# Cross-attention softmax of a decoder layer: a maximum that runs from group to group, one chunk in four subtracted by TensorE, scores in pairs of row strips

## The chip, the cores and the metric

The kernel runs on one NeuronCore of one Trainium2 chip, in one launch. The core has five engines that run side by side, each taking its own instructions in order: TensorE (PE, matrix products; its weight loads show as PEld), VectorE (DVE), ScalarE (ACT), GpSimd (POOL) and SyncE (SP, which issues the DMAs). PE writes its results to PSUM, a memory of eight banks of 128 x 512 floats; the other tiles lie in SBUF. Instructions on different engines wait for each other through semaphores.

The metric is device microseconds of one execution. Three executions of the kernel before took 688.26, 689.32 and 690.29 us, median 689.32.

## The reference

One decoder layer on 8 sequences of 128 tokens, width 512, all float32. Three residual blocks, each followed by a layer norm: self-attention with quantised weights, cross attention, and a gated mixture with low-rank experts. The change lies in the cross attention, whose softmax runs over an unusual axis:

```python
def proj(x, W, bias):                       # 16 heads of 32
    y = x @ W.T + bias
    return y.reshape(b, s, head_num, hd).transpose(0, 2, 1, 3).reshape(b * head_num, s, hd)
Q, K, V = proj(q, Wq, bq), proj(k, Wk, bk), proj(v, Wv, bv)
scores = jnp.einsum('bqd,bkd->bqk', Q, K) / sqrt(hd)
attn = jax.nn.softmax(scores, axis=0)       # over the 8*16 (sequence, head) pairs
res = jnp.einsum('bqk,bkd->bqd', attn, V)
```

So for each of the 128 x 128 (query, key) places, the maximum and the sum run over 128 score matrices: eight sequences times sixteen heads. Nothing can be weighed with its final factor before the last score matrix is there.

## The kernel before

The self-attention fills the first 510 us and isn't touched. After it come, in order, four stretches; the order of instructions on PE, DVE, ACT and POOL is the order in which the program emits them (it is written by hand; only SP's is left to a scheduler).

**Turning x.** `acc` holds the normalised residual, 8 tiles of 128 x 512. Loop `for t in range(B)` (L882) transposes each tile on PE (four 128 x 128 transposes into one PSUM bank, L878), ACT casts it to a high part `x1h` (L181) and DVE subtracts to get a low part `x1l` (L182): products run as three fast passes, high by high, high by low, low by high. Between the transposes stand units of the value projection (`vals`, L648; a unit is three products of 128 x 512 for one slice of 128 rows, four units and one bias product make one sequence). `VALUES_FIRST = 12` of the 32 units are placed here. The weights of the query projection arrive by DMA and are split on ACT and POOL in the same loop (`load_wq`, L863).

**Scores.** The 128 score matrices are dealt out in 32 chunks of four sequences by one head, and eight groups of four chunks. A chunk fills one PSUM bank: key position on the partitions, 4 x 128 (sequence, query position) along it. `cross_products` (L965) makes the four chunks of a group in one burst: a head has only 32 dimensions, so a product uses 32 of the array's 128 rows, and the inner loop walks over four heads in four different strips of 32 rows (L974). `cross_scores` (L982) takes the maximum of the four chunks: ACT copies the first to `top` (L991), DVE takes the maximum with the other three (L993). Then `close_group`: DVE reduces `top` over the four sequences to the group's maximum (L1080), subtracts that from each of the four chunks on the way from PSUM to SBUF (L1004), and ACT exponentiates in place (L1007). DVE also carries a running total maximum `mx` (L1085, L1087). The sums of the exponentials of the first six groups are made on POOL (L1013, L1019, L1020), those of group 6 by PE (products with the identity, L951), those of group 7 on DVE (L1013) and then PE.

The loop at L1093 interleaves this, chunk by chunk, with the units of the query projection of the next group (L693, four units a group) and with `VALUES_AT = (3, 3, 3, 3, 3, 3, 2)` units of the values. `SCORE_BANKS` names six banks, of which two are shared with those projections. A group's exponentials are relative to its own maximum; at the end factors exp(group maximum - total maximum) put them on one footing (L1038 to L1056).

**Factors and weighing.** PE adds up the sums (`lsum`, L951); DVE multiplies by the factors, reduces, takes the reciprocal (L1169 to L1171), forms one factor per group (L1174, L1319) and weighs the exponentials of sequences 0 and 1 (`weigh`, L1184), half of them on DVE, half on POOL (`WEIGH0_ON`, `WEIGH1_ON`, `WEIGH_ON = 'vvgg'`).

**Values and gate.** `for i in range(B)` with `AV_SEQ` (L1397): products of the exponentials with the values (`cross_values`, L1331), ACT copy, transpose (L1345), residual sum on DVE (L1347), layer norm (L222 to L230), transpose (L878), main product of the next block (L1208) and its gate (L1195), while sequence i + 2 is weighed. The rest is the mixture's end, not touched.

Of the kernel before, what the change touches and what calls it, by code (L numbers as in the profile page):

```python
# [49 lines left out]
VALUES_FIRST = 12  # L50
VALUES_AT = (3, 3, 3, 3, 3, 3, 2)
SCORE_BANKS = ('sc', 'tr', 'av', 'po', 'proj', 'proj')
EARLY_AT = 8
POPS = 2
LATE_GROUPS = (4, 4)
SUM_ORDER = (0, 1, 2)
DIRECT = (6,)
FACTORS_AT = (1, 2)
WEIGH0_ON = 'vvgg'
WEIGH1_ON = 'vvgg'  # L60
LADD_AT = 4
GSUM_ON = 'g'
# [14 lines left out]
WEIGH_ON = 'vvgg'  # L77
FIRST_WEIGHED = (2, 0, 3, 1)
# [52 lines left out]
BANKS = {"proj": 4, "sc": 1, "tr": 1, "av": 1, "po": 1}  # L131
# [7 lines left out]
def decoder_kernel(ctx: ExitStack, tc: tile.TileContext, a: dict, out: bass.AP):  # L139
# [5 lines left out]
    psum = {"n": BANKS_FIRST, "cm": tc.tile_pool(name="banks", bufs=1, space=PSUM)}  # L145
    psum["pool"] = psum["cm"].__enter__()

    def bank(tag, name, shape=(P, 512)):
        tag = tag if tag in psum["n"] else "turn"
        return psum["pool"].tile(list(shape), F32, tag=tag, name=name, bufs=psum["n"][tag])  # L150
# [449 lines left out]
    def open_cross():  # L600
# [47 lines left out]
        def vals(t):  # L648
# [4 lines left out]
            def part(kt):  # L653
                if kt == 0:
                    bk.append(bank("proj", f"pxv{t}"))
# [17 lines left out]
        for t in range(B):  # L673
            values_late.extend(vals(t))
# [10 lines left out]
    def x_projection(dst, m, w, x, hf, o):  # L685
        bk = []

        def part(kt):
            if kt == 0:
                bk.append(bank("proj", f"px{m}{hf}_{o}"))  # L690
# [177 lines left out]
    turn_n = [0]  # L868

    def other_bank(name, shape=(P, 512)):  # L870

        turn_n[0] += 1
        return bank(("sc", "tr", "av", "po")[turn_n[0] % 4], name, shape)
# [7 lines left out]
    wq_loads = []  # L881
    for t in range(B):  # L882
        n = VALUES_FIRST * (t + 1) // B - VALUES_FIRST * t // B
        for u in values_late[:n]:
            u()
        values_late = values_late[n:]
        if wq_loads:
            wq_loads.pop(0)()
        if t < KT:
            wq_loads.append(load_wq(t))  # L890
        tr = transposed(other_bank(f"tr_x1{t}", (P, KT, S)), t)
        hf, c = t // HALF, ts(t % HALF, S)
        split(x1[hf]["h"][:, :, c], x1[hf]["l"][:, :, c], tr[:])
    close(xr_cm)
# [4 lines left out]
    e_cm, ep = pool("e", "right")  # L899
    quads = {}  # L900

    def chunk(hf, m, rg):
        return (hf * KT + m) * 4 + rg

    def scores_of(c):

        k = c // 4
        if k not in quads:
            memory = {4: (e2, "x1h"), 5: (e2, "x1l"), 6: (xk["work"], "cl0"), 7: (xk["work"], "cl1")}
            if k in memory:  # L910
                pl, tag = memory[k]
                quads[k] = pl.tile([P, 4, HALF, S], F32, tag=tag, name=f"E{k}")
            else:
                quads[k] = ep.tile([P, 4, HALF, S], F32, tag=f"E{k}", name=f"E{k}")
        return quads[k][:, c % 4]

    xscale = 1.0 / math.sqrt(XD)  # L920
    LATE = len(LATE_GROUPS)
    EARLY = (2 * XH - sum(LATE_GROUPS)) // 4
    GROUPS = EARLY + LATE
    SIZES = (4,) * EARLY + LATE_GROUPS
    FIRST = [sum(SIZES[:i]) for i in range(GROUPS + 1)]
    gmax = ep.tile([P, EARLY, S], F32, name="gmax")
    gsum = ep.tile([P, EARLY, S], F32, name="gsum")
    lmax = ep.tile([P, 1 + LATE, S], F32, name="lmax")
    mx = ep.tile([P, S], F32, name="xmx")
    tops, lsum, sums, added, order, at_end = {}, [], {}, {}, list(SUM_ORDER), []  # L930

    def group_of(c):
        return next(i for i in range(GROUPS) if c < FIRST[i + 1])

    def max_of(gi):
        return gmax[:, gi, :] if gi < EARLY else lmax[:, gi - EARLY + 1, :]

    def late_sum(k, terms, n):

        sums.setdefault(k, (n, []))[1].extend(terms)  # L940

    def add_up():

        while order and order[0] in sums:
            k = order[0]
            n, terms = sums[k]
            if not lsum:
                lsum.append(bank("proj", "lsum", (P, 1 + LATE, S)))
            for x in terms:
                i = added[k] = added.get(k, -1) + 1  # L950
                nc.tensor.matmul(lsum[0][:, k, :], ident[:], x, start=(i == 0), stop=(i == n - 1))  # L951
            terms.clear()
            if added.get(k) != n - 1:
                return
            order.pop(0)
# [7 lines left out]
    burst = {}  # L963

    def cross_products(hf, m):  # L965


        for rg in range(4):
            c = chunk(hf, m, rg)
            burst[c] = bank(SCORE_BANKS[c % len(SCORE_BANKS)], f"xsc{c}", (P, HALF, S))  # L970
        for j in range(HALF):
            b = ts(hf * HALF + j, S)
            for rg in range(4):
                nc.tensor.matmul(  # L974
                    burst[chunk(hf, m, rg)][:, j, :],
                    xk["kT"][hf][ts(rg, XD), m, ts(j, S)],
                    qT[ts(rg, XD), m, b],
                    start=True,
                    stop=True,
                )  # L980

    def cross_scores(hf, m, rg):  # L982

        c = chunk(hf, m, rg)
        gi = group_of(c)
        i = c - FIRST[gi]
        if rg == 0:
            cross_products(hf, m)
        if i == 0:
            tops[gi] = xq.tile([P, HALF, S], F32, tag="top", name=f"top{gi}", bufs=1)  # L990
            nc.scalar.copy(tops[gi][:], burst[c][:])  # L991
        else:
            nc.vector.tensor_tensor(tops[gi][:], tops[gi][:], burst[c][:], ALU.max)  # L993

    def close_group(gi):

        c0, n = FIRST[gi], SIZES[gi]
        early, last = gi < EARLY, gi == GROUPS - 1
        direct = gi in DIRECT
        part = None if direct else ep.tile([P, HALF, S], F32, tag="part", name=f"part{gi}", bufs=1)  # L1000
        e = [scores_of(c0 + i) for i in range(n)]

        def minus(i):
            nc.vector.tensor_tensor(e[i], burst.pop(c0 + i)[:], across(max_of(gi)), ALU.subtract)  # L1004

        def exponential(i):
            nc.scalar.activation(e[i], e[i], AF.Exp, scale=xscale)  # L1007

        def add(i):
            if direct:  # L1010
                late_sum(gi - EARLY + 1, [e[i][:, j, :] for j in range(HALF)], n * HALF)
            elif i:
                (nc.gpsimd if early else nc.vector).tensor_tensor(  # L1013
                    part[:], e[0] if i == 1 else part[:], e[i], ALU.add
                )

        def total():
            if early:
                nc.gpsimd.tensor_tensor(part[:, :2, :], part[:, :2, :], part[:, 2:, :], ALU.add)  # L1019
                nc.gpsimd.tensor_tensor(gsum[:, gi, :], part[:, 0, :], part[:, 1, :], ALU.add)  # L1020
            else:
                late_sum(gi - EARLY + 1, [part[:, j, :] for j in range(HALF)], HALF)

        for i in range(n):
            minus(i)
        for i in range(2):
            exponential(i)

        at = max(soft[1], soft[2])
# [34 lines left out]
    def soon(n, f):  # L1064
        soft[0].setdefault(n, []).append(f)
# [579 lines left out]
```

## Time and profile before

The profiled execution took 690.76 us, 1.44 us above the median of the three; its span, from the first to the last instruction, is 688.9 us, so 1.9 us lie around it. The mean granted clock of TensorE in it is 0.977 of full speed.

| stretch | from | to | PE busy | DVE busy | ACT busy | POOL busy | clock |
|---|---|---|---|---|---|---|---|
| turning x | 514.5 | 532.5 | 17.96 of 18.0 | 9.92 | 8.82 | 7.34 | 1.00 |
| scores, groups 0 and 1 | 532.5 | 553.0 | 18.57 of 20.5 | 16.82 | 9.21 | 9.74 | 1.00 |
| scores, groups 2 to 4 | 553.0 | 575.0 | 19.90 of 22.0 | 19.65 | 11.67 | 14.55 | 1.00 |
| scores, groups 5 to 7 | 575.0 | 590.0 | 12.63 of 15.0 | 14.48 | 7.88 | 10.79 | 0.83 |
| sums, factors, weighing | 590.0 | 606.0 | 8.33 of 16.0 | 15.48 | 3.54 | 6.54 | 0.71 |
| values and gate, first five | 606.0 | 640.0 | 30.86 of 34.0 | 19.20 | 13.06 | 21.09 | 0.86 |

Times are us from the start of the span. How to read it: an engine that is busy for nearly the whole of a stretch may set its length, but a matmul's record reaches on into the next one's start (records of 0.39 us begin 0.23 us apart), so a busy PE is less full than it looks. The clock column is the share of full speed that the hardware granted to the array; 0.71 is a mean of pieces at 1.00 and pieces at 0.50. What ends a stretch is read from the chain of waits, in which each piece of work is followed back to what released it.

### The profile page before, as it was taken

The numbers are of one execution on the slowest core, as the hardware profiler recorded it, in microseconds if no ns is written. First come the engines' busy times: TensorE is split into PE (matmuls) and PEld (weight loads), VectorE is DVE, ScalarE is ACT, GpSimd is POOL, SyncE is SP. The second block draws the span as 40 slices with busy tenths as digits, with TensorE's granted clock in tenths as the row PEclk, the third lists the DMA queues.
The fourth block names the chain that finished last, engine by engine and source line by source line (L and its number), as shares of the span: only waits on it lengthen the run. The fifth ranks groups of instructions, "written<-read, shape, count | busy, mean of one in ns | idle before, by whom it ended". The sixth has DMA issues, their size and how long they took to land.

```text
span 688.9 us, 11383 instructions
## 1 busy us (share of the span) xinstructions
PE 647.6 (94%) x3476; PEld 489.1 (71%) x3476; DVE 518.4 (75%) x1319; ACT 465.5 (68%) x1181; POOL 466.2 (68%) x452
## 2 busy tenths in 40 slices
PE   6899899999999999999999999989999988579996
PEld 3787677778787777777777877757767665556652
DVE  4978676778777878788787877876894899965465
ACT  3478889987898888897888878867114455223433
POOL 4655977978879788797797887976033477366514
PEclk9999999999999999999999999989999999669999
DMA  8664432433433334343332431443001001100003
GB/s 286 182 180 116 113 84 70 108 95 89 108 92 93 85 102 93 79 111 100 78 84 47 139 77 47 114 186 115 1 0 31 1 1 62 35 2 1 1 0 123
DMA packets 31775, 57.36 MB, mean 83 GB/s; under 512 B 4831, under 2 KB 7135, under 8 KB 31714
## 3 DMA queue, kind: packets, MB, share of 16 engines
q1 hardware_dynamic: 31714, 56.64, 29.7%
q8 instruction: 27, 0.44, 0.3%
q14 instruction: 34, 0.28, 0.1%
HBM read 33.55 MB, written 2.10 MB: 52 GB/s over the span
## 4 chain that ended last, share of the span: by engine, by line
PE 73%; DVE 11%; POOL 7%; ACT 4%; issue 3%; DMA 1%; SPq 0%; POOLq 0%; DVEq 0%; ACTq 0%
PE ps L316 20%; PE po L452 15%; PE sc L383 7%; PE av L422 7%; PE ps L302 4%; PE tr L414 3%; PE pf L1208 3%; PE pxk L693 3%; PE pxv L657 2%; POOL q L351 2%; DVE top L993 2%; PE pxq L693 2%; POOL sw L350 1%; DVE E L1004 1%; PE tr_x L878 1%
## 5 line engine op out<-in xcount | busy, mean ns | idle before, releaser
L316 PE MATMUL ps<-xh,w 128*128 128x512 f32 x336 | 157.0, 467 | 0.0
L326 DVE SCALAR_TENSOR_TENSOR part<-ps,scales,part 128x512 f32<-128x512 f32 x168 | 125.7, 748 | 28.9 <-ACT part L322 19.1
L316 PE MATMUL ps<-xl,w 128*128 128x512 f32 x336 | 132.4, 394 | 0.0
L461 ACT ACTIVATE po<-po,ratios 128x512 f32<-128x512 f32 x162 | 105.0, 660 | 39.1 <-PE po L452 38.1
L349 POOL TENSOR_TENSOR t<-x,tables 128x512 f32<-128x512 f32 x70 | 90.2, 1289 | 40.6 <-DVE x L326 36.2
L452 PE MATMUL po<-ch,wo 128*128 128x512 f32 x256 | 113.7, 444 | 1.8 <-ACT accT L463 1.4
L350 POOL TENSOR_TENSOR sw<-sw,tables 128x512 f32<-128x512 f32 x71 | 92.1, 1297 | 20.1 <-DMA sw<-x 17.1
L397 ACT ACTIVATE p<-p,nmx 128x128 f32<-128x128 f32 x256 | 99.1, 391 | 4.8 <-DVE nmx L388 4.8
L452 PE MATMUL po<-cl,wo 128*128 128x512 f32 x256 | 101.4, 396 | 0.0
L351 POOL TENSOR_TENSOR q<-t,sw 128x512 f32<-128x512 f32 x62 | 81.9, 1321 | 13.0 <-DVE sw L350 8.6
L404 POOL TENSOR_TENSOR p<-p,rden 128x512 f32<-128x512 f32 x64 | 67.7, 1058 | 13.6 <-DVE rden L403 13.6
L316 PEld LDWEIGHTS ps<-xl,w 128*128 128x128 f32 x336 | 63.6, 189 | 18.7 <-issue 10.1
L316 PEld LDWEIGHTS ps<-xh,w 128*128 128x128 f32 x336 | 63.4, 189 | 18.6 <-DVE nmx L388 6.3
L383 PEld LDWEIGHTS sc<-k,q 128*128 128x128 f32 x512 | 67.3, 191 | 9.1 <-POOL q L351 3.5
L383 PE MATMUL sc<-k,q 128*128 128x128 f32 x512 | 68.7, 276 | 2.8 <-POOL q L351 2.8
L452 PEld LDWEIGHTS po<-ch,wo 128*128 128x128 f32 x256 | 48.4, 189 | 25.3 <-DVE po L459 6.2
L422 PE MATMUL av<-pt,v 128*128 128x512 f32 x128 | 66.2, 598 | 0.0
L326 DVE SCALAR_TENSOR_TENSOR x<-ps,scales,part 128x512 f32<-128x512 f32 x70 | 52.4, 749 | 14.6 <-PE ps L316 6.1
L388 DVE CUSTOM_DVE_ANT_0 p<-sc,causal 128x128 f32<-128x128 f32 x256 | 58.6, 286 | 6.3 <-PE sc L383 6.3
L322 ACT ACTIVATE part<-ps,scales 128x512 f32<-128x512 f32 x84 | 57.8, 688 | 0.0
L452 PEld LDWEIGHTS po<-cl,wo 128*128 128x128 f32 x256 | 48.7, 190 | 12.8 <-issue 4.6
L186 DVE TENSOR_TENSOR cl<-av,ch 128x512 fp32r<-128x512 f32 x64 | 44.1, 690 | 13.7 <-ACT ch L185 13.4
(247 smaller groups left out, 1294.3 us busy)
## 6 DMA issues: line engine op xcount, KB each, us to landing
sw<-x SPq DMA_DIRECT2D x160, 128.0 KB, 2.3
raw<-in_qkv SPq DMA_DIRECT2D x28, 384.0 KB, 3.1
oraw<-in_qw_o SPq DMA_DIRECT2D x32, 256.0 KB, 2.7
xraw<-in_xT SPq DMA_DIRECT2D x4, 512.0 KB, 6.4
ctxraw<-in_ctxT SPq DMA_DIRECT2D x2, 1024.0 KB, 4.9
acc<-in_x SPq DMA_DIRECT2D x8, 256.0 KB, 5.5
out<-o SPq DMA_DIRECT2D x8, 256.0 KB, 2.0
xwrawk<-in_WkT SPq DMA_DIRECT2D x1, 1024.0 KB, 5.4
```

Source lines behind the costliest of these rows:

```text
L316: nc.tensor.matmul(ps[:], w[:, kt, ts(j, HD)], x[:, kt, ts(hf, HN)], start=(i == 0), stop=(i == 1))
L326: nc.vector.scalar_tensor_tensor(to, ps[:], sc, parts[0][:], ALU.mult, ALU.add)
L349: later(delay("cos"), lambda: engine("cos").tensor_tensor(seqs(t[:]), seqs(x[:]), table(cos_t[m]), ALU.mult), True)
L350: later(delay("sin"), lambda: engine("sin").tensor_tensor(seqs(sw[:]), seqs(sw[:]), table(sin_t[m]), ALU.mult), True)
L351: later(delay("q"), lambda: engine("q").tensor_tensor(dst, t[:], sw[:], ALU.add), True)
L383: nc.tensor.matmul(sc[:, r, :], t["q"][:, r, ts(j, S)], t["k"][:, ts(j, S)], start=True, stop=True)
L388: nc.vector.tensor_tensor_reduce(out=p[:, r, :], in0=sc[:, r, :], in1=causal[:], scale=-1.0, scalar=3e38, op0=ALU.add, op1=ALU.min, accum_ ...
L397: nc.scalar.activation(p[:, r, :], p[:, r, :], AF.Exp, scale=-1.0, bias=nmx[:, r : r + 1], accum_out=den[:, r : r + 1],)
L404: nc.gpsimd.tensor_tensor(p[:], p[:], rden[:].unsqueeze(2).to_broadcast([P, REP, S]), ALU.mult)
L422: nc.tensor.matmul(av[:], t["v"][:, j, :], pt[:], start=True, stop=True)
L452: nc.tensor.matmul(ps[:], o_w[g][:, r, ts(c, P)], t["c" + m][:, r, :], start=(r == 0 and i == 0), stop=(i == 1), skip_group_check=True,)
L461: later(delay("out"), lambda: nc.scalar.activation(ps[:], ps[:], AF.Copy, scale=sc))
```

## The change

- The query projection of the first three groups moves ahead into the turning of x (`TURN_FILL`: after tiles 4, 5 and 6), and only 8 value units stay there; the other 24 are spread: one a round behind the work of each of the seven rounds, the rest behind the last group and in the first step of the values loop.
- The products of a group are made in two pairs of chunks (`products(r, pair)`): the inner loop walks over two strips of 32 rows, not four. A pair waits only for the two banks that it writes. The first pair of group r + 2 and the second of group r + 1 are made in round r. Score banks are six of their own; the query projection has one bank, the values one.
- The maximum of a group starts from that of the group before (`maxima`: the first maximum of a round takes the chunk against `gmax[r - 1]`), so that the last group's maximum is the total maximum; `mx` and its instructions on DVE go, and ACT's copy of the first chunk becomes a DVE instruction.
- In groups 0 to 6, the fourth chunk is subtracted by PE: one product of minus the identity with the maximum, added in the chunk's bank (`minus`), and ACT exponentiates straight from PSUM.
- The sums of groups 0 to 6 are all made on POOL, that of group 7 by PE (16 products). Groups 0 to 4 are put on the footing of group 5 during the rounds, so that only two factors are left at the end.
- The exponentials are weighed on DVE alone (`WEIGH_ON = 'vvvv'`); the setting up of the gate's constants moves behind the first weighing.
- Tiles move to other memory: `E6` to the keys' first half, `E7` to the queries' first half, `fw` (weights of the next block, 1 MB by DMA) to a pool of its own that opens behind the last maximum.

```diff
-VALUES_FIRST = 12
-VALUES_AT = (3, 3, 3, 3, 3, 3, 2)
-SCORE_BANKS = ('sc', 'tr', 'av', 'po', 'proj', 'proj')
-LATE_GROUPS = (4, 4)
-WEIGH0_ON = 'vvgg'
-WEIGH1_ON = 'vvgg'
+TURN_FILL = ("v", "v", "v", "vv", "vvv", "qqqq", "qqqq", "qqqq")
+SCORE_BANKS = ("sc", "tr", "pc", "pd", "av", "po")
+QUERY_BANK, VALUE_BANK = "pa", "pb"
+GROUPS = 8
+EARLY = 6
+BY_TENSOR = (1, 1, 1, 1, 1, 1, 1, 0)
+LEFT_FILL = (2, 4)
-WEIGH_ON = 'vvgg'
+WEIGH_ON = 'vvvv'
...
+    def products(r, pair):
+        hf, m = divmod(r, KT)
+        rgs = (2 * pair, 2 * pair + 1)
...
+        for j in range(HALF):
+            for rg in rgs:
+                nc.tensor.matmul(burst[4 * r + rg][:, j, :], xk["kT"][hf][ts(rg, XD), m, ts(j, S)],
+                    qT[ts(rg, XD), m, b], start=j == 0, stop=True, skip_group_check=True)
+    def maxima(r, pair):
+        for rg in (2 * pair, 2 * pair + 1):
+            if rg:
+                nc.vector.tensor_tensor(tops[r][:], tops[r][:], ps[:], ALU.max)
+            elif r:
+                nc.vector.tensor_tensor(tops[r][:], ps[:], across(gmax[:, r - 1, :]), ALU.max)
+            else:
+                nc.vector.tensor_copy(tops[r][:], ps[:])
+    def minus(r, i):
+        m = across(gmax[:, r, :])
+        if by_tensor(r, i):
+            nc.tensor.matmul(ps[:], minus_ident[:], m, start=False, stop=True, skip_group_check=True)
+        else:
+            nc.vector.tensor_tensor(scores_of(4 * r + i), ps[:], m, ALU.subtract)
+    def exponential(r, i):
+        x = burst[4 * r + i][:] if by_tensor(r, i) else e
+        nc.scalar.activation(e, x, AF.Exp, scale=xscale)
...
+        if t == B - 1:
+            products(0, 0)
+            products(0, 1)
         tr = transposed(...)
+    products(1, 0)
+    maxima(0, 0)
+    maxima(0, 1)
+    group_maximum(0)
+    for r in range(GROUPS - 1):
+        units = query_units(r + 3, QUERY_BANK) if r + 3 < GROUPS else []   # work(): one of these, or of the values left
+        minus(r, 3)
+        minus(r, 0)
+        exponential(r, 0)
+        work()
+        minus(r, 1)
+        exponential(r, 3)
+        minus(r, 2)
+        products(r + 1, 1)
+        exponential(r, 1)
+        exponential(r, 2)
...
+        work()
+        if r + 2 < GROUPS:
+            products(r + 2, 0)
+        maxima(r + 1, 0)
+        maxima(r + 1, 1)
+        group_maximum(r + 1)
+        work()
+        work()
+        fill_round(1)
+        group_sum(r)                  # POOL: three sums of 128x512, then 256, then 128
...
+        if r == EARLY:                # PE: six products of the sums with the identity
...
+    for i in range(4):
+        minus(7, i)
+        exponential(7, i)
+    fill_round(LEFT_FILL[0])          # two value units
...                                   # PE: 16 products of group 7's exponentials with the identity
+    fill_round(LEFT_FILL[1])          # four value units
...
-    for m in FIRST_WEIGHED:
-        early_inverse(m, m + 1)
-        weigh(0, m, engine_of(m, WEIGH0_ON))
...
+    for m in range(KT):
+        if m < 2:
+            inverses(*((0, 1), (1, KT))[m])
+        weigh(0, m, engine_of(m))
+    gate_constants()
+    for m in range(KT):
+        weigh(1, m, engine_of(m))
```

## The prediction

> **What bounds the kernel now.** I read the page first (PE 94% busy, the chain that ended last 73% PE and 11% DVE; the DVE lines L993, L1004 and L1080 in it are those of the cross softmax), then the chain of waits through the score loop and its end, then PE's timeline around one burst of score products, then busy time and clock by windows of 2 us.
>
> The chain, groups 3 and 4, then the end of the loop:
>
> ```profile
> 558.92 1.09 DVE gmax L1080
> 560.03 2.48 DVE E L1004 x4
> 562.51 0.34 DVE xmx L1085
> 562.86 0.68 issue
> 563.54 0.69 DVE top L993
> ...
> 566.92 0.70 DVE E L1004
> 567.63 0.14 issue
> 567.76 0.93 PE pxq L693 x3
> ...
> 592.50 0.70 DVE part L1013
> ...
> 594.83 1.17 PE lsum L951 x8
> 596.03 0.57 DVE total L1169
> ```
>
> The loop is a ring through DVE: maxima, reduction, four subtractions, the running maximum. PE comes in only where a burst waits for banks. From the first group maximum (end 537.7) to the last (589.3) it takes 51.6 us, 7.4 a group, of which DVE's own work is 5.9 plus the running maximum with its wait (0.34 + 0.68). Both DVE and PE are nearly full: PE's dense stretch from burst to burst, 554.80 to 561.60, is 6.8.
>
> One burst on PE, in the timeline (start, duration; the x8 row is the same burst in a window that closes at 532.75):
>
> ```profile
> 532.14 0.39 PE L657 MATMUL pxv<-xwvh,ctxl 128*128 128x512 f32 x1
> 532.46 1.17 PE L974 MATMUL xsc<-accT,xkT 32*128 32x128 f32 x32
> 533.56 0.50 PE L693 MATMUL pxq<-x1h,xwqh 128*128 128x512 f32 x1
> ...
> 532.46 0.50 PE L974 MATMUL xsc<-accT,xkT 32*128 32x128 f32 x8
> ```
>
> Windows that close earlier and later show four records at 532.46, four more 0.2 us later, then four every 0.11: the strips run together, in eight steps (two to a product, four products to a strip), and the last drains. Against the 0.23 us pitch of its neighbours (0.32 into the burst, 1.10 in it, 0.34 behind) a burst costs PE 1.30 us.
>
> Windows of 2 us (busy and count of PE, PEld, DVE, ACT, POOL; clock; DMA):
>
> ```profile
> 580.00:582.00 2.00, 1.53 (x6) 0.93 (x6) 1.86 (x4) 1.75 (x3) 1.92 (x2) 1.00 0.68 197
> 582.00:584.00 2.00, 1.01 (x6) 0.66 (x6) 1.97 (x4) 0.90 (x3) 1.82 (x3) 1.00 0.88 314
> 584.00:586.00 2.00, 1.26 (x27) 1.04 (x27) 2.00 (x4) 1.54 (x3) 1.94 (x2) 0.75 0.04 13
> 586.00:588.00 2.00, 2.00 (x9) 2.00 (x10) 1.79 (x4) 0.67 (x2) 1.57 (x4) 0.50 0.00 0
> ```
>
> PE idle for 1.5 of 4 us, and the clock is at half for some 7 us.
>
> **The change, part by part.** PE's prices: a unit of three projection products 0.70, a sequence's bias 0.42, four transposes 0.44, 0.1 where the kind of product changes.
>
> *The turning.* PE starts at 514.5 as before. To the transposes of tile 4 it does eight units (5.6), two biases (0.8), five tiles (2.2) and 0.4 of changes: 523.5. The first query group (2.8) needs the last low weights at its end; they were there at 526.7 before and come no later (the shorter fill lets ACT cast sooner). Three groups and two tiles end near 533.3, four chunks of products at 535.7 (2 x 1.2), tile 7 at 536.3. Then ACT's cast (0.6) and DVE's low part (0.6), ahead of the maxima in DVE's order: 537.65. Copy, three dependent maxima at 0.79, reduction 1.12: the first maximum is ready at 541.8. The copy, an operation that DVE doesn't show at this shape, lies between ACT's 0.59 and a DVE maximum's 0.69; I take 0.69. Against 537.7 before: **+4.1**.
>
> PE meanwhile makes the first pair of group 1 (its bank is tile 7's, free at 537.7) until 539.0, then its next instruction is the subtraction of chunk 3, which waits for the maximum. Everything in PE's queue waits behind it: 2.9 us idle, with 1.4 idle just before.
>
> *One round.* DVE: three subtractions at 0.60, four maxima at 0.79, reduction 1.12: 6.1. PE: four query units 2.8, a value unit 0.7, the subtraction 0.96 (no row has it; the nearest is L1208, also float32, 128 x 512, two records 0.86, and 0.1 of change; bounds 0.86, and 1.7 at half clock), and two pairs. A pair's four products per strip are still eight steps; that two strips run rather than four takes nothing off: 1.30 each, 2.6. Bounds: half a burst (0.65), if strips turn out to share something, and 1.30 plus one wait. Being nearest to what the burst's rows show, 1.30 stands. Sum 7.1: **PE now sets the round.** The 6.65 us of PE work a round before (four query units, three value units, bias, burst) become 7.1 with two value units fewer.
>
> The subtraction's wait: behind it stand the pair whose banks the DVE subtractions free, and the units. The maximum comes 5.65 us after the subtraction starts (0.96 + 0.7 + 1.3 + two maxima and a reduction), so at 7.1 a round it is always there first; ACT's exponentials (four at 0.6, one eviction at 0.7) and POOL's sums (5.3) fit in.
>
> Six rounds: 42.5, two biases 0.8, and in round 5, where value units follow each other through one bank, 0.8 for ACT's copy: 44.1. With 0.1 ahead and 5.65 behind, 49.85 from first to last maximum, at full clock.
>
> *The clock.* [...] The stretches at half speed here last 6.8 or 17 us; 3.4 to 5 us of one fall on work, which loses half: 1.7 to 2.5, **2.1** taken. So 51.95 against 51.6: **+0.4**.
>
> [...]
>
> *Behind the last maximum.* PE still has, from the start of its last subtraction: 0.96, unit, pair, unit and bias, copy wait, three units: 6.95; six products of sums 1.3; a unit and bias 1.1, copy wait 0.75, a unit 0.7 (ahead of the sum in its queue), 16 products 3.5: the sum is done 14.9 after it, 9.25 after the maximum. Before, with three additions on DVE (2.3) in the way, 6.75. **+2.5**: the saved additions are lost behind value units.
>
> *Factors, weighing.* From the sum: 0.3 + 1.0 + 0.5 for total, reciprocal, first factors, eight weighings at 0.62 and three small factors 1.0, gate constants' comparisons 0.4: 8.4 to the first residual. Before 596.0 to 606.5: 10.5, since two DVE weighings took 1.7 beside POOL's. **-2.1**. The 1 MB of weights and POOL's constants have 8 us before DVE needs the constants. The value units left over (2.5) lie under the ACT and DVE chain.
>
> *Values loop.* Its first steps ran at half clock before (598 to 614). PE is fuller now, but waits 2.9 us for the first layer norm; I count **-0.8**, bounds -2 and +1.5. Weighing on DVE adds 1.3 us a step to some 4 of 6.7, POOL loses 2.5: no change, covered by PE.
>
> Sum: 4.1 + 0.4 + 2.5 - 2.1 - 0.8 = +4.1. On the profiled execution (690.76) 694.9; on the median (689.32) **693.4**.
>
> **Rivals.**
> - *Faster: pairs cost half a burst.* PE's round is then 5.8, DVE's 6.1 sets it: first to last maximum 43.3, the sum 8.7 behind it, 7.3 less in all: 686.1. All of PE's round counts, about 14 us per us of a pair's price, so it turns at 1.0. For it: the running maximum is gone from DVE, and the 0.2 at a burst's edges might be shared by pairs. Against: seven intervals of 0.11 to 0.21 and a drain are already 1.1.
> [...]
> - *The clock drops longer or twice* (17 us, as at the end before; strips of 32 rows may count as little work): 698 to 700.
> - *The subtraction doesn't move the bound:* if DVE stays at 7.4 a round for a reason that I don't see (small DVE operations stretch to 1.1 us beside POOL's), rounds hide PE's cost: 7 x 7.4 instead of 52, the same 693.
>
> **How the numbers follow.** Chances: my sum, with or without the last rival, 0.5 (691.5 to 695.5); clock holds 0.15 (690 to 692.5); drops longer 0.2; faster by pairs or by a warm end 0.15. About 0.3%, 2.1 us, is what a measurement of this kernel tells from no change. The faster case is beyond it (0.15); the clock's case straddles it with the low edge of mine (0.15); the rest is slower (0.70). Cutting a tenth from each end: 687.8 to 698.
>
> **What would show it.** Right: pairs at 1.1 from start to drain; rounds near 7.1 with PE never idle and DVE's maxima of the second pair waiting for PE; first maximum near 542; PE idle 3 us before it and half clock after; sum 9 us behind the last maximum. Wrong: rounds near 6.1, a pair under 0.9, or a last maximum before 588.

## The result

The changed kernel takes 697.4 us (median; its executions lie between 692.3 and 700.1) against 689.6 us before: a ratio of 1.0106, with a 95% interval of 1.008 to 1.0132. So it is 7.9 us slower. The forecast was 693.4 in a range of 687.8 to 698.0, with 0.70 for slower: sign and range hold, the size is 4 us short.

The twelve executions are not all alike. Nine took 696.7 to 700.1 us at mean clocks of 0.980 to 0.984, three 692.3 to 693.7 us, two of these at 0.991 and 0.993. From the mean clocks and the spans one can estimate that these two spent 10 to 12 us at half clock, where the profiled one (0.982) spent about 25: perhaps without the stretch of 13.6 us shown below. They were not profiled.

The profiled execution of the changed kernel has a span of 695.2 us (before 688.9). Ahead of the change the two are the same program, yet the first value unit starts at 511.95 us against 514.54: in the execution of before the clock was at half for 6.8 us (458.7 to 465.5), in this one it was not. From the first value unit on, the change therefore costs 8.9 us, and it is laid out here from there:

| stretch | before | after | difference | forecast |
|---|---|---|---|---|
| first value unit to first group maximum | 23.2 | 26.4 | +3.3 | +4.1 |
| first to last group maximum | 51.6 | 54.9 | +3.3 | +0.4 |
| last maximum to the last sum | 6.7 | 9.5 | +2.8 | +2.5 |
| sum to the first residual | 10.5 | 9.0 | -1.5 | -2.1 |
| first residual to the end | 82.4 | 83.5 | +1.1 | -0.8 |

The chain of waits through the score loop (start, duration, engine, tile, line; in the changed kernel L948 is the reduction to a group's maximum, L958 the subtraction on TensorE, L926 a pair of score products, L691 and L656 units of queries and values, L1081 the sum of the last group):

```profile
537.36 1.03 DVE gmax L948
538.39 0.04 issue
538.43 2.07 PE xsc L958 x2
540.50 1.28 PE pxq L691 x3
541.78 2.01 PE xsc L926 x16
...
558.38 0.86 PE xsc L958 x2
559.24 0.69 PE pxq L691 x3
559.93 1.09 PE xsc L926 x16
561.02 0.89 PE pxq L691 x3
561.91 1.09 PE xsc L926 x16
...
599.11 3.59 PE lsum L1081 x32
...
602.82 0.29 DVE gsum L1130
603.11 0.21 DVE gsum L1131
...
603.34 0.30 DVE gsum L1132
...
603.67 0.30 DVE factor L1133
```

Where the chain of before went through DVE's maxima and subtractions, it now stays on TensorE from the first maximum to the sum. The same steps take 2.07, 1.28 and 2.01 in round 0 and 0.86, 0.69 and 1.09 in round 2. The windows of 2 us say why (busy and count of PE, PEld, DVE, ACT, POOL; then the granted clock):

```profile
534.00:536.00 2.00, 1.15 (x14) 0.96 (x14) 1.93 (x4) 0.00 (x0) 0.00 (x0) 1.00 0.00 0
536.00:538.00 2.00, 0.00 (x0) 0.00 (x0) 1.88 (x3) 0.00 (x0) 0.00 (x0) 0.91 0.00 0
538.00:540.00 2.00, 1.57 (x3) 0.84 (x3) 1.97 (x4) 0.63 (x1) 0.00 (x0) 0.50 0.00 0
...
548.00:550.00 2.00, 2.00 (x6) 1.55 (x5) 1.58 (x3) 0.00 (x0) 0.00 (x0) 0.50 0.00 0
550.00:552.00 2.00, 2.00 (x7) 1.37 (x5) 0.00 (x0) 1.21 (x2) 0.00 (x0) 0.68 0.00 0
552.00:554.00 2.00, 2.00 (x20) 1.35 (x18) 0.00 (x0) 1.63 (x3) 0.37 (x1) 1.00 0.00 0
```

TensorE waits, the clock falls to half at 537.6, and it stays there until 551.3: 13.6 us, although TensorE is busy again from 538.4 on. Round 0, from the start of its subtraction to that of the next (538.43 to 551.31), takes 12.9 us; the rounds at full clock take 6.9 (558.38 to 565.29).

What TensorE waited for between 538 and 617 us (total, times, longest):

```profile
PE tr_x L872 <- ACT acc L229: 3.5, 1, 3.5
PE xsc L958 <- DVE gmax L948: 2.7, 1, 2.7
PE pxv L656 <- ACT xv L661: 2.7, 4, 0.7
```

Three things are left in this list: the first maximum, the copies of values out of their one bank, and the first layer norm of the values loop. The experiments take them one by one.

### The profile page after: what moved, and what is told of

It reads as the page before. It is cut to its first block, busy times and chain, and to the rows that moved or that the text cites. A ratio compares the mean times of both kernels' runs of the same rounds, so it can differ in the third digit from the quotient of the medians.

```text
span 695.2 us, 11374 instructions
## 1 busy us (share of the span) xinstructions
PE 659.5 (95%) x3482; PEld 495.9 (71%) x3482; DVE 512.7 (74%) x1324; ACT 460.2 (66%) x1173; POOL 452.8 (65%) x442
## 4 chain that ended last, share of the span: by engine, by line
PE 80%; DVE 7%; POOL 6%; ACT 3%; issue 2%; DMA 1%; SPq 0%; POOLq 0%; DVEq 0%; ACTq 0%
PE ps L315 21%; PE po L451 15%; PE sc L382 7%; PE av L421 7%; PE pxq L691 4%; PE tr L413 4%; PE ps L301 3%; PE pf L1170 3%; PE xsc L926 3%; PE pxv L656 2%; PE pxk L691 2%; PE pg L1157 1%; POOL q L350 1%; POOL sw L349 1%; PE xsc L958 1%
```

## The experiments

The theory: TensorE's work sets the changed rounds; the wait for the first maximum halves the clock where TensorE is the bound; the last sum waits in TensorE's queue behind value units. Rivals stand with each run. Each ratio is to the kernel before.

| run | median us | ratio to before, 95% interval |
|---|---|---|
| e1_busy_wait | 693.3 | 1.0049 (1.0028 to 1.0071) |
| e2_unit_out | 696.4 | 1.0083 (1.0059 to 1.0106) |
| e5_one_burst | 696.1 | 1.0078 (1.0055 to 1.0100) |
| e6_no_tensor | 693.8 | 1.0050 (1.0031 to 1.0069) |
| e3_sums_first | 693.8 | 1.0045 (1.0025 to 1.0065) |
| e9_half_filled | 692.1 | 1.0040 (1.0019 to 1.0061) |
| e8_both_waits | 692.9 | 1.0039 (1.0023 to 1.0055) |
| b1_before_busy | 690.3 | 1.0011 (0.9995 to 1.0026) |
| c1_wait_filled | 691.2 | 1.0014 (0.9991 to 1.0037) |
| c4_light_rounds | 685.1 | 0.9927 (0.9902 to 0.9951) |
| c5_weigh_both | 683.3 | 0.9910 (0.9885 to 0.9936) |
| c6_light_dve | 687.2 | 0.9963 (0.9935 to 0.9992) |

### The wait and the clock

```diff
     products(1, 0)
+    warm = bank(VALUE_BANK, "warm")
+    for i in range(12):
+        nc.tensor.matmul(warm[:], wq["h"][:, 0, ts(0, P)], x1[0]["h"][:, 0], start=True, stop=True)
     maxima(0, 0)
```

> The changed kernel, with twelve more products on TensorE between the first pair of group 1 and the first subtraction; their result is never read. They fill the 2.72 us in which TensorE waits for the first group maximum (12 x 0.23 = 2.8 us at full clock); everything else is the same. Theory (the wait halves the clock, and round 0 pays for it): TensorE stays at full clock through round 0, which falls from 12.9 us to about 7; from the first to the last maximum 54.9 becomes 49, and the time falls by about 6 to some 691.5. Rival (the clock falls for another reason: the products on strips of 32 rows, or the transposes ahead of them, count as little work): the clock is halved all the same, round 0 stays near 12, and the time stays at 696 to 698.

The run took 693.3 us, 4.1 less by the medians; its profile's span is 688.9, 6.3 less. TensorE's timeline in that run:

```profile
535.98 3.03 PE L1009 MATMUL warm<-x1h,xwqh 128*128 128x512 f32 x12
538.85 1.10 PE L958 MATMUL xsc<-gmax,minus_ident 128*128 128x512 f32 x2
...
545.85 1.02 PE L958 MATMUL xsc<-gmax,minus_ident 128*128 128x512 f32 x2
```

and its windows:

```profile
538.00:540.00 2.00, 2.00 (x8) 1.18 (x7) 1.97 (x3) 0.41 (x1) 0.00 (x0) 1.00 0.00 0
540.00:542.00 2.00, 2.00 (x20) 1.46 (x19) 1.90 (x4) 1.74 (x4) 0.65 (x1) 1.00 0.04 8
```

Work that nobody reads makes round 0 take 7.0 us (538.85 to 545.85) instead of 12.9, and the first to the last maximum 49.0 instead of 54.9. So in these two profiles the wait costs 5.9 us in this stretch, none of it by being idle: the first maximum comes no earlier. The profile is of the fastest of the ten executions; by the medians it is 4.1. The rival, another reason for the half clock, falls: the products on strips and the transposes are the same, and the clock holds.

Half as much filling, against the run with twelve products:

```diff
-    for i in range(12):
+    for i in range(6):
```

> The changed kernel with six instead of twelve unread products before the first subtraction: 1.4 us of the wait of 2.72 us are filled, 1.3 us stay idle behind 1.0 us idle shortly before. [...]

The forecast was 693 to 697, spread out; 693 or less if six products do what twelve do. The median, 692.1, is with the second, yet single executions reach 697.1, with mean clocks between 0.982 and 0.996, much as with twelve products (690.7 to 696.8). In the profile 1.14 us of the wait is left, 0.99 us idle precede it, and the clock is at 1.00 in the windows of 2 us from 536 to 550. So in this profile 1.4 us of filling do what 2.8 do; where the spread comes from, this run doesn't tell.

Both waits filled, the first maximum's (with the twelve products above) and the first layer norm's:

```diff
+            if what == "A" and i == 1:
+                warm2 = bank(VALUE_BANK, "warm2")
+                for _ in range(14):
+                    nc.tensor.matmul(
+                        warm2[:], xk["c"]["h"][1][:, 3, 0, :], xk["w"]["v"]["h"][:, 0, :], start=True, stop=True
+                    )
```

> The changed kernel with products whose result is never read in two waits of TensorE: the twelve before the first subtraction (as in the run with the wait kept busy) and fourteen more (3.2 us) between the second sequence's weighed values and the first transposes of the values loop, where it waits 3.5 us for the first layer norm. Theory (the spread of the run with one wait busy, 690.7 to 696.8 with mean clocks from 0.996 to 0.982, is the clock falling at the second wait in some executions and lasting for one to four windows): the executions draw together at 689.5 to 692, with a mean clock over 0.99. Rival (the spread comes from elsewhere, such as ACT's or POOL's late work): median 693 and a spread of 5 us as before.

The spread went as the theory has it: 692.5 to 694.6, mean clocks 0.992 to 0.996, where one filled wait left 6 us of spread. The level did not: 692.9 instead of at most 692. The profile, of the slowest of the six executions, shows one cause, in TensorE's timeline ahead of the first subtraction and in the windows:

```profile
537.33 1.16 PE L926 MATMUL xsc<-accT,xkT 32*128 32x128 f32 x14 [0.99 <-DVE x1l L181]
538.41 4.61 PE L1009 MATMUL warm<-x1h,xwqh 128*128 128x512 f32 x12
```

```profile
538.00:540.00 2.00, 2.00 (x14) 1.55 (x11) 1.93 (x3) 0.00 (x0) 0.00 (x0) 0.84 0.00 0
540.00:542.00 2.00, 2.00 (x6) 1.60 (x5) 1.88 (x4) 0.01 (x1) 0.00 (x0) 0.50 0.00 0
542.00:544.00 2.00, 2.00 (x7) 1.29 (x6) 1.90 (x4) 0.71 (x2) 0.00 (x0) 0.80 0.00 0
```

The same twelve products take 4.61 us, not 3.03: the clock of 0.84, 0.50 and 0.80 is one stretch of 3.4 us at half, after a gap of only 0.99 us. In the run with twelve products alone the same gap was there and the clock held.

### What sets the rounds

One value unit less in rounds 0 to 4:

```diff
-        fill_round(1)
+        fill_round(1 if r >= EARLY - 1 else 0)
```

> The changed kernel without the value unit at the end of rounds 0 to 4: five units of 0.70 us move behind the rounds (eight are left for the values loop, three before). Theory (TensorE's work sets the round): rounds 1 to 4 become 0.7 shorter (6.9 to 6.2, where DVE's own 6.1 takes over), round 0 at half clock about 1.3; the first to last maximum falls from 54.9 to about 51. Of these 4 us the values loop gives some back, because the five units (3.5 us) come there ahead of its first transposes: 693.5 to 697. Rival (DVE's ring of maxima sets the round and TensorE is full only because units are put there): rounds stay at 6.9, TensorE shows idle time instead, and the time is 697 or more.

The rounds at full clock fell from 6.9 to 6.4 us (565.34 to 571.73) and the first to the last maximum to 51.2, 3.6 less. From the first value unit to the end the profile is 3.2 us shorter (180.1 against 183.3): the moved units stand in the way of the values loop (from the first residual to the second 8.0 us instead of 7.2). By the medians the time fell by only 1.1, to 696.4; there are four executions of this run, and why the medians show less than the profiles is open. That a round shrinks when TensorE's work is taken out of it speaks for the theory. It shrinks by 0.5 and not by 0.7. The trace has a candidate for the missing 0.2: the first query unit of a round now starts when ACT's copy of the previous units out of the same bank ends (559.13 and 0.69 us; the product starts at 559.87), 0.94 us behind the subtraction instead of 0.46. No run separates it.

The pairs undone, those of the first group too:

```diff
-    products(1, 0)
     maxima(0, 0)
...
-        products(r + 1, 1)
+        products(r + 1, 0, 1)
...
-        if r + 2 < GROUPS:
-            products(r + 2, 0)
```

> The changed kernel with the two pairs of each group made as one burst of four chunks again (group 1's burst and later ones stand behind the second DVE subtraction, as their four banks come free then; the subtraction on TensorE and the running maximum stay). Theory (a pair costs what a burst costs, and that is why TensorE sets the round): TensorE's round falls by one pair, 1.09, to 5.8, but DVE now waits for the burst: two subtractions 1.2, burst 1.1 to 1.3, four maxima 3.2, reduction 1.1, about 6.8 to 7.0 a round with TensorE idle some 1 us in it. The rounds gain nothing or little, 696 to 698 if the clock falls as before, up to 4 more if the short waits keep it low. Rival (a pair costs less than a burst, edges aside): the burst takes near 2.2 us, rounds 7.5 or more, over 701.

696.1 us, and rounds of 7.1 us. A burst of four strips in this run, in TensorE's timeline (the start of the next product gives its price):

```profile
559.23 1.17 PE L926 MATMUL xsc<-accT,xkT 32*128 32x128 f32 x32
560.33 0.50 PE L691 MATMUL pxq<-x1h,xwqh 128*128 128x512 f32 x1
```

A pair of two strips in the changed kernel:

```profile
559.86 1.16 PE L926 MATMUL xsc<-accT,xkT 32*128 32x128 f32 x16
560.95 0.50 PE L691 MATMUL pxq<-x1h,xwqh 128*128 128x512 f32 x1
```

1.10 us for 32 products, 1.09 for 16: half the products cost the same. What the pairs buy is on DVE; in the run with one burst each round has this:

```profile
567.54 0.69 DVE L943 TENSOR_TENSOR top<-xsc,gmax 128x512 f32<-128x512 f32 x1 [1.07 <-PE xsc L926]
```

DVE waits 1.07 us for the burst, TensorE 1.2 us for the maximum. Pairs take the wait from DVE and give TensorE 1.09 us more work: 7.1 becomes 6.9. Two strips cost what four do (1.09 and 1.10), and a step of a burst takes 0.11 us, as does one of four transposes on all 128 rows (0.44 together). Two pairs right behind each other, on different strips, take 1.65 us ahead of the last tile's transposes (32 records, 530.85 to 532.50), not 2 x 1.09: they overlap in part.

The subtraction on TensorE undone:

```diff
-BY_TENSOR = (1, 1, 1, 1, 1, 1, 1, 0)
+BY_TENSOR = (0, 0, 0, 0, 0, 0, 0, 0)
```

> The changed kernel with all four subtractions of every group on DVE and none on TensorE; pairs, running maximum and order of the units stay. TensorE's round loses 0.86 (6.9 to 6.05), DVE's gains a subtraction of 0.60 (6.1 to 6.7, and 0.2 to 0.5 of waits for the second pair). Theory (TensorE sets the changed rounds, by no more than 0.2 to 0.4 over what DVE would need with the fourth subtraction): rounds 6.75 to 7.1, and the half-clock round 0 is 1.7 shorter; the wait before the first maximum still halves the clock, as TensorE has only one unit before it waits for DVE's subtractions: 694.5 to 698, so that the subtraction on TensorE bought nothing. Rival (DVE sets the rounds, and the subtraction on TensorE is a saving of 0.6 a round): rounds 7.5, 701 or more.

693.8 us, 3.6 less than the changed kernel and a little below what the theory allowed. The maxima's reductions on DVE, in rounds at full clock:

```profile
562.83 1.08 DVE L948 TENSOR_REDUCE gmax<-top 128x128 f32<-128x512 f32 x1
...
569.43 1.09 DVE L948 TENSOR_REDUCE gmax<-top 128x128 f32<-128x512 f32 x1
```

6.6 us a round with all four subtractions on DVE, 6.9 with one on TensorE; round 0, still at half clock (its units' products begin 0.43 us apart, later ones 0.23), is shorter too, and the first to the last maximum takes 50.6. So beside a value unit in each round the subtraction on TensorE costs 0.3 us a round rather than saving 0.6.

### Behind the last maximum

```diff
-LEFT_FILL = (2, 4)
+LEFT_FILL = (0, 6)
```

> The changed kernel with the two value units that stand ahead of the last 16 sum products put behind them. Theory (the last sum waits for TensorE's queue and not for the exponentials, which are done 2.5 us before it starts): the sum products start when the twelve for the earlier groups end, at 596.1 rather than 599.0, so the sum is 2.9 us earlier, and the first residual too; the units that move lie beside DVE's factors and weighings, 9 us: about 694.5. Rival (the units cost the same wherever they stand, because the values of the first sequences or the copies on ACT hold the values loop): 697.

693.8 us, 3.7 less. TensorE in that run:

```profile
596.53 1.50 PE L1056 MATMUL lsum<-gsum,ident 128*128 128x128 f32 x12
597.86 3.74 PE L1081 MATMUL lsum<-accT,ident 128*128 128x128 f32 x32
```

The last sum starts 8.3 us after the last subtraction on TensorE (589.53), where it was 11.1; the first residual follows 21.4 instead of 23.9 us behind that subtraction. The two units cost nothing behind the sum.

### Versions that use the idle time

The query units of group 3 fill the wait for the first maximum, and no value unit stands in rounds 0 to 3:

```diff
     products(1, 0)
+    for u in query_units(3, QUERY_BANK):
+        u()
...
-        units = query_units(r + 3, QUERY_BANK) if r + 3 < GROUPS else []
+        units = query_units(r + 4, QUERY_BANK) if r + 4 < GROUPS else []
...
-        fill_round(1)
+        fill_round(1 if r >= 4 else 0)
```

with the sums first (`LEFT_FILL = (0, 6)`).

> The changed kernel with useful work in the wait: the four query units of group 3 (2.8 us) stand between the first pair of group 1 and the first subtraction, later groups of query units one round earlier; no value unit in rounds 0 to 3 (four of them in round 4, in the place of its query units); sum products ahead of the value units that are left, as in the run with the sums first. Theory: the clock stays full (the run with unread products there was 4.1 us faster by the medians, 6.3 by the profiles), rounds 0 to 3 take 6.4 instead of 6.9 (2 us), the sum is 3.7 earlier as measured: 697.4 - 4.1 - 3.7 - 2 = 687.6, between 685.5 and 690. Rival (gains of the same stretch cancel, because the units only move from one place on the path to another): 690 to 693.

The median of 691.2 misses the forecast and lies in the rival's range. The profile speaks against the rival's reason, though: the rounds did shrink. Single executions go from 687.1, at a mean clock of 0.997, to 695.5 at 0.982. In the profile (span 686.8) rounds 0 to 3 take 6.4 us at full clock. What is missing goes with the clock: the wait for the first layer norm is still there, and behind it the clock falls even in this rather quick execution:

```profile
608.00:610.00 2.00, 0.72 (x6) 0.67 (x7) 0.33 (x1) 1.30 (x3) 0.38 (x1) 1.00 0.00 0
610.00:612.00 2.00, 1.79 (x10) 1.56 (x9) 1.49 (x3) 0.56 (x1) 0.00 (x0) 0.71 0.00 0
612.00:614.00 2.00, 2.00 (x28) 1.57 (x30) 1.90 (x7) 0.58 (x2) 1.19 (x2) 0.50 0.00 0
```

That the long executions lose more in the same place is argued from the run with both waits filled; they were not profiled.

No value unit in any round, the values in two banks in turn, and what is left of the units in the wait for the first layer norm (against the run above):

```diff
-        fill_round(1 if r >= 4 else 0)
...
-    left = [u for t in range(2, B) for u in xk["vals"](t, VALUE_BANK)]
+    left = [u for t in range(2, B) for u in xk["vals"](t, (VALUE_BANK, QUERY_BANK)[t % 2])]
...
         for what in AV_SEQ:
             step(what, i, state)
+            while what == "A" and i == 1 and fill:
+                fill.pop(0)()
-        while fill:
+        while i and fill:
             fill.pop(0)()
```

> As the run with the wait filled, and also no value unit at the end of any round, the value units' banks in turn (the query units' bank is free by then, so no wait of 0.68 for ACT's copy), and what is left of the units behind the second sequence's weighed values, where TensorE waits 3.5 us for the first layer norm. Theory (what stands in the rounds is on the path, what stands in that wait is not): rounds 4 to 6 fall by 0.5 to 0.7 each and two copy waits of 0.68 go, so 2 to 3 us less than the run with the wait filled: 684 to 687. Rival (the units only move; the values loop starts later by as much): the same time as the run with the wait filled, within 1 us.

685.1 us, faster than the kernel before (0.9927); 6.1 less than the run with the wait filled, where 2 to 3 were expected. From the first value unit to the end the two profiles differ by 2.9 us (170.0 against 172.9), as expected; the rest of the medians' difference goes with the clock, which is 0.993 to 0.998 in all executions here and went down to 0.982 there. The first to the last maximum takes 46.4 us, with one half-clock stretch of 3.4 us in it after the 0.99 us gap, as above.

Two of a sequence's four weighings in the values loop back on POOL:

```diff
-            weigh(i + 2, m, engine_of(m))
+            weigh(i + 2, m, engine_of(m, 'vvgg'))
```

> As the run with light rounds, with two of a sequence's four weighings on POOL in the values loop, as before the change (the first two sequences' are weighed as in the change, on DVE). Theory (POOL's small operation of the first layer norm took 1.33 us instead of 0.27 because DVE weighed beside it, and DVE's four weighings in a row delay the first layer norm): 0.5 to 1.5 us less than the run with light rounds. Rival (POOL is late with the weighings itself, 2 x 1.1 us and more beside DVE's, and the layer norm's small operations queue behind them on POOL): the same or up to 2 us more.

683.3 us, the fastest: 0.991 of before. What the weighing itself is worth is not shown. The intervals of this run and the last overlap. Their profiles differ by 1.6 us from the first value unit on, and that difference lies between the first and the last maximum (44.8 against 46.4), where the run before had its half-clock stretch; from the last maximum to the end they differ by 0.2 (96.8 against 97.0).

What did change is an operation on POOL. In the changed kernel POOL's second small operation of the first layer norm and of the next were:

```profile
614.67 1.33 POOL L228 TENSOR_SCALAR nmr_x<-mv_x,rstd_x 128x1 f32<-128x1 f32 x1
...
621.84 0.26 POOL L228 TENSOR_SCALAR nmr_x<-mv_x,rstd_x 128x1 f32<-128x1 f32 x1
```

The first one ends at 616.0, when DVE's four weighings in a row end (613.46 and 2.49 us). With two of them on POOL it is short:

```profile
601.26 0.27 POOL L228 TENSOR_SCALAR nmr_x<-mv_x,rstd_x 128x1 f32<-128x1 f32 x1
601.49 2.52 POOL L1148 TENSOR_TENSOR E<-E,gmax 128x512 f32<-128x512 f32 x2
```

The operation of 1.33 us ends with DVE's row, but the POOL operation just before it took 0.88 us beside the same row, against 0.93 elsewhere: why the one is long and the other is not stays open. One window of 62 us in this version's profile:

```profile
538.00:600.00 62.00, 61.65 (x435) 42.53 (x437) 54.19 (x87) 24.68 (x45) 40.69 (x53) 1.00 0.09 28
```

TensorE is busy for 61.65 of 62 us at full clock, from ahead of the first subtraction (539.17) into the values loop.

The same version with all four subtractions on DVE (`BY_TENSOR` all zeros, as above):

> As the run with light rounds and the weighing on both engines (683.3), with all four subtractions of each group on DVE. Theory (there TensorE has 0.2 us a round less work than the round lasts, and with four subtractions on DVE the round was 6.6, as in the run without the subtraction on TensorE): rounds 6.6 instead of 6.4, 1.3 us more, 684 to 686; so the subtraction on TensorE pays only once the value units are out of the rounds. Rival (TensorE's work sets the rounds still): rounds fall to 6.1 or less, 679 to 682.

687.2 us: 3.9 more than with the subtraction on TensorE, where 1.3 was expected. The rounds are 6.6 us, as expected. The rest is put down to the clock, from a profile of one of the slower executions (690.7 us): TensorE now has gaps in every round (it waited four times for ACT's query copies, 3.1 us in all, and twice for DVE's subtractions, 1.3), and late in the loop:

```profile
582.00:584.00 2.00, 1.15 (x7) 0.59 (x6) 2.00 (x4) 1.14 (x3) 1.92 (x3) 1.00 0.00 0
584.00:586.00 2.00, 2.00 (x15) 1.73 (x16) 1.79 (x4) 1.39 (x3) 1.56 (x2) 0.60 0.04 8
586.00:588.00 2.00, 2.00 (x6) 1.56 (x5) 1.86 (x3) 0.00 (x0) 1.84 (x3) 0.50 0.00 0
```

The clock is at half for about 10 us in all here (9.6 by the windows from 584.4 to 594.0, and the last sum behind them takes 4.25 us to the next product, 3.49 with the sums first), and the sums of the earlier groups then take 2.93 us (1.60 in the version with the subtraction on TensorE). How much of the medians' 3.9 us is the clock's was not separated.

### What the half clock cost the kernel before

```diff
+            if what == "A" and i == 0:
+                warm(18)
             step(what, i, state)
+            if what == "A" and i == 1:
+                warm(10)
```

> The kernel before, with products whose result is never read where TensorE waits at the end of the cross attention: 18 of 0.23 us ahead of the first weighed values (4.6 us idle) and 10 ahead of the first transposes of the values loop (2.45 us idle). It asks what the stretch at half clock there (17 us) cost the kernel before. Theory A (TensorE's steps there lie on the path of the first layer norms: transposes 1.1 for 0.6, gate products 2.5 for 1.3, weighed values 2.0 for 1.0): 1.5 to 3 us less, 686.5 to 688. Theory B (the weighings on DVE and POOL set that stretch, as the chain of waits says): no change, 689 to 690.5.

690.3 us against 690.25 in the same session: no change. The stretch of 17 us at half clock is down to 3.4. TensorE in that run:

```profile
593.12 4.37 PE L1400 MATMUL warm<-xwvl 128*128 128x512 f32 x18
...
608.38 0.60 PE L878 MATMUL tr_x<-ident,acc 128*128 128x128 f32 x4
...
613.56 0.66 PE L878 MATMUL tr_x<-ident,acc 128*128 128x128 f32 x4 [1.54 <-ACT acc L230]
```

The first transposes take 0.60 instead of 1.12 us and the gate products 1.35 instead of 2.50, but from the start of the last sum to the second transposes it is 21.4 us (592.20 to 613.56) against 21.9 before: TensorE now waits 1.54 us for the layer norm instead of 0.40. Where DVE and POOL set the time, half clock costs 0.5 us in these profiles and nothing by the medians; in the changed kernel's score loop it costs 5.9 us.

## Why the prediction was right, and where it was short

- *TensorE becomes the bound of the rounds, at 7.1 us.* Right: 6.9, with TensorE busy throughout. A pair's price ("1.30 each", of it 1.10 and edges) measured 1.09 and 0.2. Taking a unit out shortened the rounds.
- *The clock.* The step that failed: "3.4 to 5 us of one fall on work, which loses half: 1.7 to 2.5, 2.1 taken". That the wait halves the clock was right, the length was not. No run shows this wait followed by only 3.4 to 5 us of work at half clock, which was the author's estimate: in the changed kernel it stayed at half for 13.6 us, 12.9 of them with TensorE busy, and cost 5.9 by the profiles (4.1 by the medians). The stretch was sized from 6.8 us elsewhere in the profile, with the other length that this profile had (17 us) put into a rival at 0.2. Had the term been 5.9, the forecast would have been 697.2. That this is so near to 697.4 is partly luck: the other terms missed by -0.8, -0.8, +0.3, +0.6 and +1.9, about 1 us together, and the 8.9 us of the profiles are 1 us more than the medians show. Why the stretch was 13.6 us long is open.
- *The turning, +4.1.* Measured +3.3: the two pairs of group 0 were counted at 2 x 1.2 us, and took 1.65 together.
- *Rounds at full clock.* Against before 49.0 - 51.6 = -2.6 (from the run with the wait kept busy), where the forecast had 49.85 - 51.6. So the change does shorten the loop; the clock takes it back twice over.
- *Behind the last maximum, +2.5.* Near: +2.8, but partly by luck. The durations named in the prediction add up to 14.3 us and not to the 14.9 that it gives; by them the term is +1.9. From the last subtraction on TensorE (587.99) to the end of the sum (602.70) it was 14.7. With the units behind the sums the time fell by 3.7, so "the saved additions are lost behind value units" holds.
- *Factors and weighing, -2.1.* -1.5. The eight weighings took 5.0 us, as counted (8 x 0.62). What was too small is the total, 0.3: it takes four small operations on DVE, 1.15 us together (602.82 to 603.97, in the chain above).
- *Values loop, -0.8.* Wrong in sign: +1.1. The half clock that was to be saved there had cost 0.5 us at most before, and POOL's small operation (1.07 us longer beside DVE's weighings) and a second half-clock stretch (6.8 us, from 616), behind the 3.5 us wait, came on top; their shares were not separated. The bounds of the step, -2 to +1.5, did hold it.
- *Rivals.* "Clock holds" (690 to 692.5) is what the run with the wait kept busy made: 693.3 by the median, against 691.3 if the clock's 2.1 are taken off the forecast. "The clock drops longer" is what happened in kind: 13.6 us and 697.4, where it had 17 us and 698 to 700. The main sum's own range, 691.5 to 695.5, was missed. "Faster, if a pair costs half a burst" is excluded by 1.09 against 1.10. "The subtraction doesn't move the bound" (DVE holds a round at 7.4) is excluded by rounds of 6.9, and of 6.4 with a unit less on TensorE.

How long a wait has to be to halve the clock, no run settles. In the changed kernel 2.72 us, behind 0.99 a little earlier, did. The unit out and the sums first have the same program up to there, and their rounds show it: 8.0 and 9.6 us, and 8.0 and 10.3, from the first maximum to the second and on to the third, as 8.0 and 10.3 in the changed kernel, where the round after these takes 6.4, 6.9 and 6.9. A gap of 0.99 us alone was followed by half clock in two profiles (both waits filled, light rounds). In the run with half the filling, 0.99 and 1.14 us dropped nothing.

## What to carry to other kernels

Price a wait by what follows it: an idle TensorE may cost more after the wait than in it, if TensorE is the bound there (2.72 us of waiting, then 5.9 us by the profiles), and next to nothing if it isn't (0.5 us by the profiles in the kernel before, none by the medians). When work moves onto the engine that is already full, take as much off it in the same stretch; here the subtraction paid only once the value units had left the rounds (683.3 against 687.2, of which the rounds, 6.6 against 6.4, explain about 1.4), and cost time before that (697.4 against 693.8). Filler belongs where the engine waits (before the first maximum, behind the last sum, ahead of the first layer norm), not at the end of each round.

## What the runs showed of the hardware

- The stretches at half clock in these profiles lasted 3.4 us or a multiple of it: 3.4 (both waits filled), 6.8 (the kernel before, from 458.7; half the filling, from 612.5), about 10 (light rounds with DVE's subtractions), 13.6 (the changed kernel), 17.1 (the kernel before, from 598.6). In the changed kernel it lasted for 13.6 us with TensorE busy for all but the first 0.8. A longer gap did not cost more: with one burst TensorE had no work for at least 4.6 us before the first maximum (DVE takes the last transposes' cast at 536.18, the maximum ends at 540.74), and the next maximum came 9.6 us later, where the rounds behind it take 7.1; after 2.72 us in the changed kernel it was 8.0 and 10.3, then 6.9. These are single profiles.
- A gap of 0.99 us was followed by one such stretch in two profiles (both waits filled; light rounds) and by none in others with the same instructions ahead of it (wait kept busy; weighing on both engines). What decides no run here shows.
- The time at which the first value unit starts varies from 511.9 to 515.0 us over the profiles, with the same instructions ahead. In windows of 20 us, five profiles show no clock below 1.00 up to there, and lie at 511.9 to 512.9; all others show one stretch at half clock (before: two of them in a row, 6.8 us) and lie at 513.5 to 515.0. A difference of 2 us between two single profiles of this kernel is therefore no evidence on a change; it has to be taken from a landmark just ahead of it.
